# Last batch of an attention kernel: TensorE sums the last pieces of two halves, GpSimd and ScalarE put out two halves, the turned sums get buffers of their own, the last scores come in another order

## The chip, the cores and the metric

One core of one Trainium2 chip. The metric is the device time of one execution in microseconds (us); the time before is the median of three runs. TensorE is PE (its weight loads PEld), VectorE is DVE, ScalarE is ACT, GpSimd is POOL, and SyncE, which here only issues DMAs, is SP.

## The reference

For each of 32 images of 256 channels by 32x32 positions: a group normalisation (32 groups), projections to queries, keys and values of 8 heads with 32 channels each, attention in which a position sees only earlier positions, and the input added to the result. All in float32.

```python
q = einsum('oc,bcs->bos', q_w, gn(x)) + q_b;  kv likewise; k, v = split(kv)
scores = einsum('bhqd,bhkd->bhqk', q, k) / sqrt(32)          # S = 1024 positions
attn = softmax(where(mask == 0, -1e4, scores)); attn = where(mask == 0, 0, attn)
out = x + einsum('bhqk,bhkd->bhqd', attn, v)
```

## The kernel before

An image is a batch of the kernel. Its 8 heads are two groups g of four heads (128 channels), and its 1024 query positions are two halves hf of 512. So there are four halves per batch, n = 2g + hf = 0 to 3. Scores stand with the keys on the partitions: for a block of 128 keys, a head's scores are a 128x512 product. The exponentials (`e`, or `eh` where only 256 queries are concerned) are multiplied with the values into the numerator `acc`, and their sums over all keys are the denominators.

The program is a list of visits, 12 to a batch. Visit v of the last batch is program visit 372 + v, here written v0 to v12, v12 being the one after its last. The engines' order is written by hand (`manual_schedule`; SP's queue is not in it): each visit issues, in this order,

- its scores and exponentials and masks (`scores`: PE L269, ACT L324 twice and L322, POOL L283),
- the work listed in `at` for that visit (projections of the next image, L156, and so on),
- the products with the values of the visit before (`values`: PE L347), and on DVE the additions of those exponentials into one running sum per half (L353),
- the work listed in `after` for that visit.

Each engine works strictly in that order, so an instruction that waits holds everything behind it on its engine.

For all batches but the last, the running sum of a half is folded over the partitions by POOL's and SP's DMAs (`fold`, `stack`), turned and reduced on DVE (`sum_folded`, L382 and L383, two calls of two heads), inverted (`invert`), sent to memory and back as a broadcast tile `rb` (L425, L430), and used in `finish` (DVE L464, L465, for hf 0 also L467, then a DMA out from SP). For the batch before the last, `sum_folded` falls to v6 and v7, `invert` to v8, `finish` of its halves 0 and 1 to v10 and v11, and `finish_aside` of its halves 2 and 3 (POOL L475 and L476, ACT L477, for hf 0 L479, DMA) to v12.

The last batch has no time for that path. `sums` lets PE sum the running sum over the keys into `pd` (L390) and ACT copies it to `den` (L409); `invert_here` turns it on DVE (L450 into `turned`), checks its range (L413, L414 into `in_range`), inverts (L454) and spreads it (L455); `finish` follows. Halves 0, 1, 2 have `sums` at v3, v7, v9 and `invert_here` at v4, v8, v11; halves 0 and 1 have `finish` at v4 and v8. For half 3, `sums` comes at v11, the pieces of the last visit are summed by PE directly (`sum_piece` at v12), and `end_last` inverts it in two parts and puts out halves 3 and 2. At the end a minimum over `in_range` (L489) is summed by PE (L491) and decides whether a slower path has to run.

`den` and `turned` share one tag of the pool `small` with two buffers, in this order of use on their engines:

```python
turned = small.tile([P, HALF], F32, tag="den", ...)          # sum_folded, invert_here
live["den", n] = small.tile([P, HALF], F32, tag="den", ...)  # sums
```

PSUM has three 2-bank tiles for scores, one bank `acc`, and one bank `misc`, which `pd` shares with projections (`spare`). The tile of inverses of the last batch's half 0 has tag `rb` (4 buffers, shared with the batch before); those of halves 1 to 3 lie in `rb_last`.

In the last visit's scores, products of heads 2 and 3 for the short piece (`first`) come after the first block of the long piece, whose second block has only 128 queries.

Of the kernel before, what the change touches and what calls it, by code (L numbers as in the profile page):

```python
# [9 lines left out]
F32 = mybir.dt.float32  # L10
# [7 lines left out]
P = 128  # L18
HD = 32
# [12 lines left out]
def tile_norm_attention_residual(  # L32
# [54 lines left out]
    avg = avg.rearrange("p a b -> p (a b)")  # L87
    in_range = const.tile([P, ROW], F32, name="in_range")
    nc.gpsimd.memset(in_range, 1.0)
    eps = const.tile([P, 1], F32, name="eps")  # L90
    nc.gpsimd.memset(eps, 1e-5)

# [4 lines left out]
    def unshifted():  # L97
# [192 lines left out]
        def scores(b, full, half):  # L290


            tag = "e0" if full[2] == 0 else "e"
            name = f"{b}_{full[0]}_{full[1]}_{full[2]}"
            e = epool.tile([P, 4, HALF], F32, tag=tag, bufs=4 if tag == "e0" else 3, name=f"{tag}_{name}")
            eh = epool.tile([P, 4, HALFBANK], F32, tag="eh", bufs=4, name=f"eh_{name}")
            pairs = [ps_s.tile([P, 2, HALF], F32, tag="sT", name=f"sT_{name}_{a}") for a in range(3)]
            short = pairs[2].rearrange("p bank (n q) -> p bank n q", n=2)
            last = b == B - 1 and full[:2] == (NG - 1, NH - 1) and half[2] == NB - 2

            first = [] if last else [scores_of((b, half), short[:, j % 2, 1, :], j) for j in (2, 3)]


            for n in range(len(full[4])):
                for j in range(4):
                    scores_of((b, full), pairs[j // 2][:, j % 2, :], j, n)
                first = first or [scores_of((b, half), short[:, j % 2, 1, :], j) for j in (2, 3)]

            for ins in first:
                ins.then_inc(bank_free, 1)  # L310
                tc.no_tile_sem_insts.add(ins.ins.name)
            live["free"] = live.get("free", 0) + len(first)
            wait = nc.tensor.wait_ge(bank_free, live["free"])
            for ins in first:
                tc.declare_no_dep(wait.ins, ins.ins, reason="the semaphore orders them")
            for j in range(2):
                lo = scores_of((b, half), short[:, j, 0, :], j)
                for ins in first:
                    tc.declare_no_dep(lo.ins, ins.ins, reason="the semaphore orders them")
            for a in range(3):  # L320
                if a == 2:
                    exp = nc.scalar.activation(eh.rearrange("p (n bank) q -> p bank n q", n=2), short, AF.Exp)  # L322
                else:
                    nc.scalar.activation(e[:, 2 * a : 2 * a + 2, :], pairs[a], AF.Exp)  # L324

            for ins in first:
                tc.add_to_no_dep_group(f"first_{name}", ins.ins)
                tc.add_to_no_dep_group("first", ins.ins)
            tc.declare_no_dep(exp.ins, group=f"first_{name}", reason="through the last two products")
            tc.declare_fence(exp.ins, group=f"first_{name}")  # L330
            for heads in (range(2), range(2, 4)) if last else (range(4),):
                mask(full, e, slice(heads.start, heads.stop))
            mask(half, eh)
            live["e", b, full], live["e", b, half] = e, eh

        def values(b, pc, summed=True):
            g, hf, k, part, blocks = pc
            first, last = k == 0, k == hf * BPH + (1 if hf == 0 else 2)
            e = live.pop(("e", b, pc))
            if first:  # L340
                live["acc"] = ps_o.tile([P, HALF], F32, tag="acc", name=f"acc_{b}_{g}_{hf}")
                live["sum", b, g, hf] = e
            acc = live["acc"]
            for kb, cols, of in blocks:
                for j in range(4):
                    h = 4 * g + j
                    nc.tensor.matmul(  # L347
                        acc[HD * j : HD * (j + 1), of], lhsT=live["v", b][:, kb, h * HD : (h + 1) * HD],
                        rhs=e[:, j, cols], start=first, stop=last, skip_group_check=True,
                    )  # L350
                if not first and summed:
                    total = live["sum", b, g, hf]
                    nc.vector.tensor_add(total[:, :, of], total[:, :, of], e[:, :, cols])  # L353
            if last and (b, g, hf) == (B - 1, NG - 1, NH - 1):
# [22 lines left out]
        def sum_folded(b, heads):  # L377
            if heads.start == 0:
                live["rows", b] = small.tile([P, ROW], F32, tag="rows", name=f"rows_{b}")
            for j in heads:  # L380
                turned = small.tile([P, HALF], F32, tag="den", name=f"turned_{b}_{j}")
                nc.vector.transpose(turned, live["folded", b][:, j, :])  # L382
                nc.vector.tensor_reduce(  # L383
                    live["rows", b][:, j * HALF // HD : (j + 1) * HALF // HD],
                    turned.rearrange("p (k r) -> p k r", r=HD), AX.X, ALU.add,
                )
# [5 lines left out]
                    start=start, stop=stop, skip_group_check=True,  # L392
                )

        def sum_piece(b, pc, stop=False):

            e = live["e", b, pc]
            for kb, cols, of in pc[4]:
                sum_keys(live["den", 3], e, cols, of, False, stop)

        def sums(b, n):

            pd = misc(f"pd_{b}_{n}")
            sum_keys(pd, live.pop(("sum", b, *divmod(n, NH))), slice(0, HALF), slice(0, HALF), True, n < 3)
            if n == 3:
                live["den", n] = pd
            else:
                live["den", n] = small.tile([P, HALF], F32, tag="den", name=f"den_{b}_{n}")
                nc.scalar.copy(live["den", n], pd)  # L409

        def check_sums(rows):
            ok = in_range[:, : rows.shape[1]]
            nc.vector.scalar_tensor_tensor(ok, rows, SUM_MIN, ok, ALU.is_ge, ALU.mult)  # L413
            nc.vector.scalar_tensor_tensor(ok, rows, SUM_MAX, ok, ALU.is_le, ALU.mult)  # L414

        def invert(b):
            rows = live["rows", b]
            check_sums(rows)
            inv = small.tile([P, ROW], F32, tag="inv", name=f"inv_{b}")
            nc.vector.reciprocal(inv, rows)  # L420
            turned = small.tile([P, ROW], F32, tag="inv_turned", name=f"inv_turned_{b}")
# [21 lines left out]
        def invert_here(b, n, within=slice(0, HALF)):  # L443
# [2 lines left out]
            if within.start == 0:  # L446
                inverses(b, n)
            k = (within.stop - within.start) // HD
            turned = small.tile([P, HALF], F32, tag="den", name=f"turned_{b}_{n}_{within.start}")[:, : k * HD]
            nc.vector.transpose(turned, live["den", n][:, within])  # L450
            rows = turned.rearrange("p (k r) -> p k r", r=HD)[:, :, 0]
            check_sums(rows)
            inv = small.tile([P, ROW], F32, tag="inv", name=f"inv_{b}_{n}_{within.start}")[:, :k]
            nc.vector.reciprocal(inv, rows)  # L454
            nc.vector.transpose(  # L455
                live["rb", b, n][:, within].rearrange("p (k r) -> p k r", r=HD),
                inv.unsqueeze(2).broadcast_to([P, k, HD]),
# [9 lines left out]
                nc.vector.tensor_copy(rb[:, 0:1], xt[:, g, 0:1])  # L467
            nc.sync.dma_start(out=x_out[b, :, g, cols], in_=rb)

        def finish_aside(b, n):  # L470

            g, hf = divmod(n, NH)
            cols = slice(hf * HALF, (hf + 1) * HALF)
            rb, xt = live["rb", b, n], live["x", b]
            nc.gpsimd.tensor_tensor(rb, live["num", b, n], rb, ALU.mult)  # L475
            nc.gpsimd.tensor_tensor(rb, rb, xt[:, g, cols], ALU.add)  # L476
            nc.scalar.activation(rb, rb, AF.Identity, bias=v_bias_col[:, g : g + 1])  # L477
            if cols.start == 0:
                nc.scalar.copy(rb[:, 0:1], xt[:, g, 0:1])  # L479
            nc.sync.dma_start(out=x_out[b, :, g, cols], in_=rb)  # L480

        def end_last(b):

            both = [slice(c * HALFBANK, (c + 1) * HALFBANK) for c in range(2)]
            for part in both:
                invert_here(b, 3, part)

            worst = const.tile([P, 1], F32, name="worst")
            nc.vector.tensor_reduce(worst, in_range, AX.X, ALU.min)  # L489
# [47 lines left out]
        with tc.manual_schedule(engines={ENG.PE, ENG.Activation, ENG.DVE, ENG.Pool}):  # L537
# [31 lines left out]
            for b in range(B):  # L569
# [19 lines left out]
                elif not last:  # L589

                    for n in every[:2]:
                        when(first + N + 10 + n, lambda b=b, n=n: finish(b, n), after)
                    for n in every[2:]:
                        when(first + 2 * N, lambda b=b, n=n: finish_aside(b, n), after)
                else:
                    for n in every[:3]:
                        v = first + SUMS[n]
                        when(v, lambda b=b, n=n: sums(b, n), after)
                        v += 1 + n // 2
                        when(v, lambda b=b, n=n: invert_here(b, n), after)  # L600
                        if n < 2:
                            when(v, lambda b=b, n=n: finish(b, n), after)
            for i in range(B * N + 1):
                if i < B * N:
                    scores(i // N, *visits[i % N])
# [3 lines left out]
                if i == B * N:  # L609

                    for n, pc in enumerate(pcs):
                        sum_piece(B - 1, pc, stop=n == 1)
                for pc in pcs:
                    values((i - 1) // N, pc, i < B * N)
                if i == B * N - 1:
                    sums(B - 1, 3)
                for f in after.pop(i, ()):
                    f()
            assert not at and not after
# [158 lines left out]
```

## Time and profile before

| what | us |
|---|---|
| median of three runs | 1839.12 (1838.89 to 1840.98) |
| the profiled execution's own time | 1839.79 |
| its span | 1838.1 |
| PE busy / DVE busy / ACT busy / POOL busy | 1814.4 / 1663.4 / 1480.1 / 802.9 |
| mean granted TensorE clock | 0.993 |

The span runs from the first to the last instruction of one profiled execution; 1.69 us of the execution lie outside it, and the execution was 0.67 us over the median. The last batch's v0 starts at about 1756 us, v4 at 1775.8 and its last work on DVE ends at 1833.04; all the change is in that stretch. Busy shares over the whole span say little about it.

### The profile page before, as it was taken

The page shows a single profiled execution, that of the slowest core. Times are in us where ns is not written, and L with a number is a line of the kernel's source. Part 1 is how long each engine was busy: PE and PEld are TensorE (multiplying, and loading weights), DVE is VectorE, ACT ScalarE, POOL GpSimd, SP SyncE. Part 2 cuts the span into 40 slices and gives each one's busy share as a digit, 9 for nine tenths or more (in the row PEclk, how much of TensorE's full clock was granted, in tenths as well). Part 3 has the DMA queues.
Part 4 walks back from the last instruction along what each step waited for, and adds up shares of the span by engine and source line. Part 5 has one row for each costly group of instructions (what it writes and reads, how often), then busy time and mean ns, then how long its engine had stood idle before and what let it go on. Part 6 is the DMA issues. An engine that isn't in the chain of part 4 may idle for free.

```text
span 1838.1 us, 53791 instructions
## 1 busy us (share of the span) xinstructions
PE 1814.4 (99%) x23144; PEld 926.9 (50%) x23144; DVE 1663.4 (90%) x1774; ACT 1480.1 (81%) x1862; POOL 802.9 (44%) x779
## 2 busy tenths in 40 slices
PE   9999999999999999999999999999999999999995
PEld 5455555555555555554555555555545555555542
DVE  4799999999999999999999999999999999999988
ACT  5888878888878888888888788887888887888873
POOL 1453443534434434434445344354344454453432
PEclk9999999999999999999999999999999999999997
DMA  3457666676676666766676766667666767667651
GB/s 121 70 90 138 137 147 120 122 141 135 139 145 118 129 134 139 145 124 121 136 138 135 156 112 127 135 139 145 131 119 132 142 134 150 115 124 139 115 108 66
DMA packets 77781, 235.00 MB, mean 128 GB/s; under 512 B 20320, under 2 KB 21344, under 8 KB 61664
## 3 DMA queue, kind: packets, MB, share of 16 engines
q0 software_dynamic: 15872, 97.53, 38.7%
q1 hardware_dynamic: 61664, 133.96, 24.5%
q8 instruction: 183, 3.00, 0.7%
q14 instruction: 62, 0.51, 0.1%
HBM read 66.85 MB, written 34.57 MB: 55 GB/s over the span
## 4 chain that ended last, share of the span: by engine, by line
PE 97%; DVE 2%; issue 0%; DMA 0%; ACT 0%; DVEq 0%; ACTq 0%
PE sT L269 31%; PE acc L347 26%; PE pp L156 26%; PE ppv L156 13%; DVE e L353 1%; DVE rb L465 0%; DMA x<-in_x_dram 0%; PE pv L156 0%; PE pd L390 0%; DVE rb L464 0%; DVE st L166 0%; PE wt L135 0%; PE busy L142 0%; DVE turned L450 0%; PE pm L156 0%
## 5 line engine op out<-in xcount | busy, mean ns | idle before, releaser
L324 ACT ACTIVATE e<-sT 128x1024 f32<-128x1024 f32 x768 | 744.8, 1022 | 271.4 <-PE sT L269 213.2
L353 DVE TENSOR_TENSOR e<-e,e 128x1536 f32<-128x1536 f32 x382 | 642.3, 1681 | 17.9
L353 DVE TENSOR_TENSOR e<-e,eh 128x1024 f32<-128x1024 f32 x383 | 528.1, 1393 | 125.8 <-PE acc L347 105.3
L283 POOL TENSOR_SCALAR_AFFINE_SELECT e<-e 128x512 f32<-128x512 f32 (+1 forms) x257 | 378.5, 1473 | 575.9 <-ACT e L324 572.7
L269 PE MATMUL sT<-q,k 32*128 32x256 f32 (+3 forms) x7168 | 608.2, 459 | 0.0
L269 PEld LDWEIGHTS sT<-q,k 32*128 32x128 f32 x7168 | 445.3, 184 | 155.4 <-ACT eh L322 65.0
L156 PE MATMUL pp<-xn,wT 128*32 128x512 f32 x4096 | 494.0, 600 | 1.0 <-ACT den L409 1.0
L347 PE MATMUL acc<-e,v 128*32 128x512 f32 (+2 forms) x4096 | 401.2, 486 | 0.0
L322 ACT ACTIVATE eh<-sT 128x1024 f32<-128x1024 f32 x384 | 396.6, 1033 | 0.0
L369 POOL DMA_DIRECT2D e<-e x248 | 203.1, 823 | 388.9 <-DMA e<-e 306.5
L156 PE MATMUL ppv<-wT,xn 128*32 128x256 f32 x4096 | 247.5, 382 | 0.0
L347 PEld LDWEIGHTS acc<-e,v 128*32 128x32 f32 x4096 | 133.0, 110 | 224.6 <-issue 193.3
L347 PE MATMUL acc<-eh,v 128*32 128x256 f32 x3072 | 224.4, 379 | 0.0
L156 PEld LDWEIGHTS pp<-xn,wT 128*32 128x32 f32 x4096 | 107.2, 109 | 221.8 <-issue 206.5
L347 PEld LDWEIGHTS acc<-eh,v 128*32 128x32 f32 x3072 | 98.5, 110 | 164.2 <-issue 152.6
L156 PEld LDWEIGHTS ppv<-wT,xn 128*32 128x32 f32 x4096 | 120.1, 109 | 102.9 <-issue 30.8
L283 POOL TENSOR_SCALAR_AFFINE_SELECT eh<-eh 128x512 f32<-128x512 f32 x128 | 168.1, 1313 | 0.2
L209 ACT ACTIVATE xn<-x,shift,rstd 128x512 f32<-128x512 f32 x124 | 103.1, 831 | 0.0
L465 DVE SCALAR_TENSOR_TENSOR rb<-rb,v_bias_col,x 128x512 f32<-128x512 f32 x123 | 94.1, 765 | 4.4
L223 ACT ACTIVATE k<-pp,qk_bias 128x512 f32<-128x512 f32 x128 | 89.5, 700 | 3.2 <-PE pp L156 2.0
L223 ACT ACTIVATE q<-pp,qk_bias 128x512 f32<-128x512 f32 x128 | 89.8, 702 | 2.6 <-PE pp L156 2.6
L383 DVE TENSOR_REDUCE rows<-turned 128x16 f32<-128x512 f32 x124 | 85.0, 686 | 4.3
(70 smaller groups left out, 669.7 us busy)
## 6 DMA issues: line engine op xcount, KB each, us to landing
e<-e POOLq DMA_DIRECT2D x124, 512.0 KB, 6.2
x<-in_x_dram SPq DMA_DIRECT2D x64, 512.0 KB
out_dram<-rb SPq DMA_DIRECT2D x125, 256.0 KB
e<-e POOLq DMA_DIRECT2D x124, 256.0 KB, 4.8
folded<-e SPq DMA_DIRECT2D x124, 256.0 KB
rb<-inverses SPq DMA_DIRECT2D x124, 256.0 KB
inverses<-inv_turned SPq DMA_DIRECT2D x124, 8.0 KB
wn<-in_L_conv_kv_w_dram SPq DMA_DIRECT2D x2, 256.0 KB
```

Of the source, the lines that this page charges most:

```text
L156: nc.tensor.matmul(out[part], lhsT=lhsT[:, part], rhs=rhs, start=start, stop=stop, skip_group_check=True)
L209: nc.scalar.activation(xn, xt, AF.Identity, bias=live["shift", b][:, g : g + 1], scale=rstd)
L223: nc.scalar.activation(live[key][:, cols], pp, AF.Identity, bias=qk_bias[:, n, g : g + 1], scale=(SCALE, 1.0)[n],)
L269: return nc.tensor.matmul(pair[:, cols], lhsT=live["k", b, g][rows, kb * P : (kb + 1) * P], rhs=live["q", b, g][rows, hf * HALF + of.start ...
L283: nc.gpsimd.affine_select(out=diagonal, in_=diagonal, pattern=[[0, heads.stop - heads.start], [0, n], [1, P]], compare_op=ALU.is_gt, fill= ...
L322: exp = nc.scalar.activation(eh.rearrange("p (n bank) q -> p bank n q", n=2), short, AF.Exp)
L324: nc.scalar.activation(e[:, 2 * a : 2 * a + 2, :], pairs[a], AF.Exp)
L347: nc.tensor.matmul(acc[HD * j : HD * (j + 1), of], lhsT=live["v", b][:, kb, h * HD : (h + 1) * HD], rhs=e[:, j, cols], start=first, stop=l ...
L353: nc.vector.tensor_add(total[:, :, of], total[:, :, of], e[:, :, cols])
L369: nc.gpsimd.dma_start(out=total[:rows], in_=total[rows : 2 * rows], accum_op=ALU.add)
L383: nc.vector.tensor_reduce(live["rows", b][:, j * HALF // HD : (j + 1) * HALF // HD], turned.rearrange("p (k r) -> p k r", r=HD), AX.X, ALU ...
L465: nc.vector.scalar_tensor_tensor(rb, rb, v_bias_col[:, g : g + 1], xt[:, g, cols], ALU.add, ALU.add)
```

## The change

In the last batch:

- `values` no longer adds on DVE at v6 (the last pieces of half 1), v11 and v12 (the last of half 3; v12 was without already). `sums(1, products[5])` at v7 and `sums(3, pcs)` at v11 let PE sum those pieces from their exponentials, beside the running sum.
- `invert_here` of half 0 moves from v4 to v6 (ahead of the products), of half 2 from v11 to v10; half 1's stays at v8.
- Halves 0 and 1 are put out by `quotient_aside` (POOL, at v7 and v8) and `out_aside` (ACT and DMA, at v8 and v10) in place of `finish` on DVE.
- `turned` has a tag with two buffers of its own, `den` has one.
- The range check of the four halves becomes one over their inverses, 128x64, in `end_last`.
- `finish` of halves 0 and 1 of the batch before moves from v10 and v11 to v11, both.
- In the last visit the two short products come after half of the long piece's second block.

```diff
+    inv_last = const.tile([P, 4, HALF // HD], F32, name="inv_last")
@@ scores
+                long_of(range(4), 0)
+                long_of((0, 1), 1)
+                first = short_of((2, 3), 1)
+                long_of((2, 3), 1)
@@ values
-                if not first and summed:
+                if not summed:
+                    continue
+                if not first:
                     total = live["sum", b, g, hf]
                     nc.vector.tensor_add(total[:, :, of], total[:, :, of], e[:, :, cols])
@@ sum_folded, invert_here
-                turned = small.tile([P, HALF], F32, tag="den", ...)
+                turned = small.tile([P, HALF], F32, tag="turned", ...)
@@ sums
+        def sums(n, pcs=()):
+            live["pd"] = misc(f"pd_{n}")
+            sum_keys(live["pd"], live.pop(("sum", B - 1, *divmod(n, NH))), ..., n < 3 and not pcs)
+            for k, pc in enumerate(pcs):
+                sum_piece(pc, n < 3 and k == len(pcs) - 1)
...
+                live["den", n] = small.tile([P, HALF], F32, tag="den", bufs=1, name=f"den_{n}")
@@ invert_here
-            check_sums(rows)
-            nc.vector.reciprocal(inv, rows)
+            inv = inv_last[:, n, within.start // HD : within.stop // HD]
+            nc.vector.reciprocal(inv, turned.rearrange("p (k r) -> p k r", r=HD)[:, :, 0])
@@ quotient_aside, out_aside (finish_aside in two)
+            nc.gpsimd.tensor_tensor(rb, live["num", b, n], rb, ALU.mult)
+            nc.gpsimd.tensor_tensor(rb, rb, live["x", b][:, g, hf * HALF : (hf + 1) * HALF], ALU.add)
...
             nc.scalar.activation(rb, rb, AF.Identity, bias=v_bias_col[:, g : g + 1])
@@ end_last
+            check(inv_last.rearrange("p n k -> p (n k)"), 1.0 / SUM_MAX, 1.0 / SUM_MIN)
@@ the program
-                        when(first + N + 10 + n, lambda b=b, n=n: finish(b, n), after)
+                        when(first + N + 11, lambda b=b, n=n: finish(b, n), after)
...
-                    for n in every[:3]:
-                        v = first + SUMS[n]
-                        when(v, lambda b=b, n=n: sums(b, n), after)
-                        v += 1 + n // 2
-                        when(v, lambda b=b, n=n: invert_here(b, n), after)
-                        if n < 2:
-                            when(v, lambda b=b, n=n: finish(b, n), after)
+                    when(first + 3, lambda: sums(0), after)
+                    when(first + 7, lambda: sums(1, products[5]), after)
+                    when(first + 9, lambda: sums(2), after)
+                    for n, v in enumerate((6, 8, 10)):
+                        when(first + v, lambda b=b, n=n: invert_here(b, n), (at, after)[n > 0])
+                    for n in every[:2]:
+                        when(first + 7 + n, lambda b=b, n=n: quotient_aside(b, n), after)
+                        when(first + 8 + 2 * n, lambda b=b, n=n: out_aside(b, n), after)
@@
-                    values((i - 1) // N, pc, i < B * N)
+                    values((i - 1) // N, pc, i - (B - 1) * N not in (6, 11, 12))
                 if i == B * N - 1:
-                    sums(B - 1, 3)
+                    sums(3, pcs)
```

## The prediction

> **What bounds the kernel now.** First the page: PE is busy 99% of the span, so only what stops PE, or what lies behind PE's last work, can be worth anything. The chain of waits is PE until v4 of the last batch and then leaves it. These are its pieces (start, length, what):
>
> ```profile
> 1779.20 1.09 PE acc L347 x13
> 1780.30 1.51 DVE e L353
> ...
> 1794.06 1.24 DVE e L353
> 1795.30 0.04 issue
> 1795.34 1.98 PE pd L390 x8
> ...
> 1799.75 0.70 DVE rows L383
> ...
> 1800.55 0.59 ACT den L409
> 1801.15 0.04 issue
> 1801.19 3.64 PE pp L156 x16
> ```
>
> From 1780.30 to 1833.04, DVE's end, the chain is mostly DVE. PE's `pd` at v7 waits for DVE's last addition of v6; then ACT's copy of `pd` waits for a reduction (L383) that has nothing to do with its data. The answer on the tile `turned` names that wait, 7.5 us, once: the copy's buffer is one of the two that `turned` uses too. Behind it on ACT stand v8's exponentials, and behind the bank `misc` PE's projection.
>
> The stretches of time (PE, PEld, DVE, ACT, POOL busy with counts, granted clock, DMA share, GB/s) show the price:
>
> ```profile
> 1788.00:1791.70 3.70, 3.70 (x44) 1.77 (x40) 3.49 (x3) 3.13 (x5) 2.50 (x3) 1.00 0.01 2
> 1791.70:1795.30 3.60, 0.04 (x4) 0.00 (x0) 3.46 (x4) 1.33 (x2) 1.23 (x1) 0.89 0.00 0
> 1795.30:1801.20 5.90, 4.82 (x26) 2.00 (x26) 5.76 (x9) 0.65 (x2) 0.00 (x0) 0.50 0.00 0
> 1801.20:1804.70 3.50, 3.50 (x20) 0.88 (x24) 3.38 (x6) 2.70 (x3) 0.00 (x0) 0.50 0.05 9
> 1804.70:1816.90 12.20, 12.17 (x140) 5.79 (x132) 11.73 (x16) 9.63 (x12) 2.00 (x2) 1.00 0.28 104
> 1816.90:1820.80 3.90, 0.00 (x0) 0.00 (x0) 3.80 (x3) 0.80 (x1) 3.90 (x3) 1.00 0.23 87
> 1820.80:1833.10 12.30, 5.53 (x58) 2.39 (x58) 11.74 (x26) 1.64 (x3) 6.30 (x5) 0.68 0.21 78
> ```
>
> PE stands still for 3.60 us, then runs at half clock until 1804.7 (16 projections take 3.64 us, 1.86 elsewhere), and stands still again for 3.9 us at v11. DVE has almost no idle time in any row.
>
> **What the skill says.** The Trainium skill, "TensorE: Matmul & The Clock Gate", What's actually happening: after an idle window of about 3.4 us PE runs at half clock until it has been busy for as long. The trace agrees: clock 0.50 behind the wait of 3.60 us; gaps under 1.1 us in the chain don't do it. "SBUF — State Buffer", SBUF: two separate sides: a GpSimd operation and a DVE operation with two SBUF inputs exclude each other for a whole instruction. The trace shows interference, not that it is total: beside POOL's L475 and L476 two DVE checks of 128x16 took 0.51 and 1.21 us, 0.18 elsewhere. "GPSIMD Engine Reference", Engine selection: two-input elementwise work is about twice as slow there; here 1.49 us (mean of L475) against DVE's 0.69 (L464).
>
> **DVE's part.** From the timeline of DVE, starts to next start:
> - v6's additions go: 1790.41 to 1795.30, 4.9 us. v11's go: 1816.74 to 1820.78, 4.0.
> - output of half 0 goes (L464, L465, L467): 1783.80 to 1786.19, 2.4; of half 1: 1807.40 to 1808.80, 1.4.
> - range checks go: 0.32, 0.32, 1.75 (the one slowed by POOL), 0.36, 0.37, together 3.1; one check of 128x64 comes, as at 1801.81: 0.4.
>
> Sum 15.4 us less on DVE. Were DVE never to wait and never slowed, it would end at 1833.04 - 15.4 = 1817.6. That is the floor.
>
> **PE's and ACT's part.** Until v7's products end (1791.7) PE doesn't wait for DVE and nothing changes. `sums(1)` now needs the running sum only through v5. DVE is through with that at 1781.8 + 3.8 = 1785.6, because half 0's inversion and output no longer stand ahead of it (1781.73 to 1786.19). So `pd` starts at 1791.7: 0.86 us for the running sum (the chain's pd x8 of 512 columns at full clock) and 1.29 for 768 columns of pieces, to 1793.9. ACT ended v7's exponentials at 1793.0; with its own buffer the copy runs at once, to 1794.5. **Both waits go, and with them the reason for the half clock.** Next, with durations of full-clock rows:
> - v8: scores 1.5, projection 1.86, products 0.87: PE at 1798.1. ACT: exponentials 1795.05 (1.2 behind the scores, as at v4 and v6) to 1797.9, `k` and `num` to 1799.05, then the new L477 and L479 (0.72 + 0.19) to 1800.0. Their wait is for POOL's half 0, which starts behind v7's mask (1793.4) and takes 1.49 + 1.43, up to 3.3: 1796.7 at the latest, so no wait.
> - v9: exponentials 1800.0 to 1802.8, 0.7 later than without the new pair, and v10's short scores wait for that bank: PE loses 0.7. Products 1.72, `pd` 0.86, copy to 1803.4.
> - v10: scores to 1804.35, exponentials to 1806.9, products to 1805.6; then L477 of half 1 to 1807.6. POOL has half 1 ready at 1800.5 + 3.3 = 1803.8.
> - v11: scores (bank free at 1806.9) to 1807.9; exponentials 1807.6 to 1810.45; products to 1809.2; `sums(3)` with 768 columns of pieces (2.15) to 1811.35. The new order of scores lets pair 0 go some 0.3 us earlier, which ACT's L477 hides: I cost it at nothing, and if that cover were gone it would gain up to 0.3.
> - v12: three masks on POOL. Alone 0.94 each and 1.1, contended 1.88, 1.88 and 1.65 as at 1815.93: they end between 1811.6 and 1814.0. The pieces' sums behind them: `pd` is complete at about 1813.7.
>
> DVE beside it, from 1785.6: inversion 0 1.75, first fold turn 2.75, v7's addition (waits for `acc` to 1791.1) 1.2, second turn 2.75, `invert` 1.15, v8's additions 2.45, inversion 1 1.75, v9's 2.4, v10's 3.8, inversion 2 1.75, `finish` of two halves 3.0: 1811.4. Two things slow it. POOL's four new operations last 5.8 us; in v12 of before, POOL's four (1821.3 to 1827.25) cost DVE 2.7 (inversion 2 took 3.4 instead of 2.05, a `finish` 2.8 instead of 1.45), so 2.7; masks some 0.5. DVE is then free at 1814.6, 0.9 later than `pd`. The sum for half 3 isn't delayed: v10's additions end at 1809.4 at worst against 1809.2.
>
> **The end.** `end_last` took 1826.85 to 1833.04, 6.2; minus 0.73 of checks plus 0.4 is 5.9. It now lies wholly beside POOL's last four operations, where only 0.4 of it did: plus 2.7. DVE ends at 1814.6 + 8.6 = 1823.2. POOL's last output (1814.0 + 6.0, ACT 0.7) is at 1820.7, earlier. Behind DVE's end come 5.06 us to the span's end as before: 1828.3. With 1.69 outside, 1830.0 against this execution's 1839.79: 9.8 less; on the median, 1829.3. Rounding toward the floor's side, since a part of the POOL slowdown was counted at its worst: **1829.0 us**, a likeliest range of 1824 to 1833. Without any contention `pd` would be complete at 1812.2 and DVE end 5.9 later, 1818.1: 1824.2 on the median.
>
> **What costs nothing, and its cover.** `rb` has four buffers, and half 0's stays in use until v8's DMA out, while the batch before asks for four at v8: one of its four broadcasts (L430) must wait for that DMA. It lands by 1800.5 + 5 (5.06 is the bound that the end of the span gives), the broadcast takes at most the 10.2 us from 1804.90 to its use at 1815.09: 1815.7. If it is half 3's, POOL wants it at about 1817 and nothing waits; if half 0's, `finish` at v11 waits up to 5 us. SP's order is not written by hand, so I keep that in the range. Holding `e` of v5 until v7 costs nothing: its buffer comes round at v10.
>
> **Rivals.** (a) GpSimd's lock is total for its new work. Then the eight POOL operations cost DVE their whole 11.7 us instead of 5.4: 1829.0 + 6.3 = 1835.3; half of it, or a late broadcast, gives 1832 to 1834. For it: the 1.21 us check. Against: two DVE transposes beside them (L450, L455) kept their 0.70. (b) **Slower**: ACT's L477 of half 1 stands ahead of v11's exponentials and waits for POOL. Every us that POOL ends half 1 after 1806.9 is added to exponentials, masks, sums and end. From 1817 on the gain is used up; with POOL starved to 1820, 1842. Against: POOL's operations took at most 1.69 with DVE busy throughout, and would need five times that. (c) The waits go, but DVE stays behind PE at `sums(2)` and `sums(3)`, PE idles over 3.4 us there and falls to half clock again: about 6 us back and the `pd` of v12 twice as long, 1837, which a measurement cannot tell from no change (0.2%, 3.7 us, is about its limit).
>
> **Numbers.** Likeliest case 0.77, (a) 0.13, (c) 0.04, (b) 0.06. Faster by over 0.2%: 0.90; within: 0.04; slower: 0.06. The range reaches from the uncontended 1824 to most of (a): 1824.0 to 1834.5.
>
> **What would show it.** Right: no PE wait for L353 at v7 and none of ACT for L383; clock near 1.0 until v12; `pd` at v7 with 32 products; v8's projection at 1.9 us; DVE's additions 5 fewer; DVE idle for less than 2 us ahead of half 3's inversion; span near 1827. Wrong: DVE idle for long at v8 to v11 (ACT or POOL is the bound), an idle PE of over 3 us anywhere before v12, an L430 issued long after the other three, or DVE operations doubled beside L475.

## The result, and the profile after

| | before | changed | ratio (95% interval) |
|---|---|---|---|
| median of six runs each, us | 1839.63 (1838.79 to 1840.98) | 1828.07 (1827.45 to 1829.07) | 0.9938 (0.9925 to 0.9950) |
| profiled execution: time, span, us | 1839.79, 1838.1 | 1827.53, 1825.8 | |
| from v4's first scores product to the end of the span, us | 62.33 | 51.52 | |

The forecast was 1829.0, within 1824.0 to 1834.5. The last row is the one to compare kernels by. Of the 12.3 us between the two spans, 1.49 lie before v4 (scores at 1775.77 and 1774.28), where the change has no work. They are not the change's: three variants of the changed kernel that are profiled below (with the old order of scores, without POOL's work of v12, and with v10's pieces on PE and another buffer) began v4 at 1775.75 to 1776.06, as the kernel before did. PE's clock between 9 and 12 us of the span was 0.55 in one of the two profiles and 1.00 in the other; in the fourteen profiles of this case it was 0.51 to 0.60 in seven, with v4 at 1775.7 to 1776.1, and 1.00 in seven, with v4 at 1774.2 to 1774.6 in all but one. So the change is worth 10.81 us in the profiles. The stretch from v4's first scores product to the end of the span is called the tail below.

The changed kernel has other line numbers for the same work: L356 stands for L347 of before (products with the values), L364 for L353 (additions), L393 and L394 for L382 and L383, L401 for L390 (`pd`), L425 for L409 (copy to `den`), L445 for L430 (broadcasts), L465, L467 and L468 for L450, L454 and L455 (inversion), L477, L478 and L480 for L464, L465 and L467 (`finish`), L487 and L488 for L475 and L476 (POOL), L494 for L477 (ACT), L428 and L429 for the checks L413 and L414.

The stretches of the changed kernel (PE, PEld, DVE, ACT, POOL busy with counts, clock, DMA share, GB/s). All times in it are 1.49 us earlier than in the kernel before for the same work:

```profile
1788.00:1791.70 3.70, 3.70 (x55) 1.70 (x52) 2.79 (x4) 2.97 (x4) 1.39 (x2) 1.00 0.02 7
1791.70:1795.30 3.60, 3.60 (x52) 1.84 (x45) 3.46 (x7) 2.36 (x3) 2.94 (x3) 1.00 0.00 0
1795.30:1801.20 5.90, 5.90 (x78) 2.81 (x70) 5.76 (x9) 5.87 (x10) 1.29 (x1) 1.00 0.19 62
1801.20:1804.70 3.50, 3.50 (x44) 1.89 (x36) 3.40 (x2) 3.04 (x5) 3.42 (x3) 1.00 0.33 124
1804.70:1809.40 4.70, 4.04 (x46) 1.92 (x44) 4.53 (x5) 3.47 (x5) 4.70 (x4) 1.00 0.18 63
1809.40:1813.00 3.60, 3.60 (x64) 1.74 (x56) 3.53 (x5) 0.00 (x0) 3.52 (x3) 1.00 0.38 126
1813.00:1820.80 7.80, 0.45 (x10) 0.12 (x2) 7.42 (x19) 1.64 (x3) 3.10 (x3) 0.80 0.44 160
```

PE is busy without a break until 1804.7 and idle for 0.66 us after that, the clock is 1.00 to 1813.0, PE's last products but a few, and ACT, which did 0.65 us in 5.9 before, now does 5.87. The chain of waits of the changed kernel (start, length, what) shows where it leaves PE now:

```profile
1790.25 2.15 PE pd L401 x32
1792.41 1.50 PE sT L270 x12
1793.91 1.85 PE pp L157 x16
...
1799.75 3.40 DVE e L364 x2
...
1803.25 3.19 DVE e L364
...
1810.36 1.66 DVE rb L478
...
1812.20 1.51 DVE rb L477
...
1814.49 0.37 DVE turned L465
```

`pd` of v7 follows PE's products at once, with 32 products in 2.15 us, and v8's projection takes 1.85 (3.64 before). From 1799.75, the additions at v9, the chain is DVE to DVE's end, 21.1 us of it. Its length is not its work: two additions of 128x1024 that took 2.35 us in the kernel before, with POOL idle, took 3.40. The timelines of before (two lines) and of the changed kernel (four) show these additions and those that follow, with POOL's work on half 1 beside them:

```profile
1808.80 2.35 DVE L353 TENSOR_TENSOR e<-e,eh 128x1024 f32<-128x1024 f32 x2
1811.26 2.29 DVE L353 TENSOR_TENSOR e<-e,e 128x2048 f32<-128x2048 f32 x1
...
1799.75 3.40 DVE L364 TENSOR_TENSOR e<-e,eh 128x1024 f32<-128x1024 f32 x2
1799.91 2.15 POOL L487 TENSOR_TENSOR rb_last<-num,rb_last 128x512 f32<-128x512 f32 x1 [5.19 <-DVE rb_last L468]
1802.14 2.14 POOL L488 TENSOR_TENSOR rb_last<-rb_last,x 128x512 f32<-128x512 f32 x1
1803.25 3.18 DVE L364 TENSOR_TENSOR e<-e,e 128x2048 f32<-128x2048 f32 x1
```

### The profile page after: what moved, and what is told of

Its sections match the earlier page's. It is cut to its first block, busy times and chain, and to the rows that moved or that the text cites. A ratio compares the mean times of both kernels' runs of the same rounds, so it can differ in the third digit from the quotient of the medians.

```text
span 1825.8 us, 53853 instructions
## 1 busy us (share of the span) xinstructions
PE 1809.1 (99%) x23184; PEld 925.3 (51%) x23184; DVE 1652.5 (91%) x1756; ACT 1481.7 (81%) x1865; POOL 808.8 (44%) x783
## 3 DMA queue, kind: packets, MB, share of 16 engines
q0 software_dynamic: 15872, 97.53, 38.8%
## 4 chain that ended last, share of the span: by engine, by line
PE 98%; DVE 1%; DMA 0%; ACT 0%; issue 0%; DVEq 0%
PE sT L270 31%; PE acc L356 27%; PE pp L157 26%; PE ppv L157 13%; DVE e L364 0%; DMA x<-in_x_dram 0%; PE pv L157 0%; PE pd L401 0%; DVE st L167 0%; DVE rb L478 0%; DVE rb L477 0%; PE pm L157 0%; DVE rb_last L478 0%; DVE rb_last L468 0%; PE busy L143 0%
## 5 line engine op out<-in xcount | busy, mean ns | idle before, releaser
L364 DVE TENSOR_TENSOR e<-e,e 128x1536 f32<-128x1536 f32 (+1 forms) x379 | 636.9, 1680 | 17.8
L364 DVE TENSOR_TENSOR e<-e,eh 128x1024 f32<-128x1024 f32 x381 | 526.9, 1397 | 124.9 <-PE acc L356 104.1
L356 PE MATMUL acc<-e,v 128*32 128x512 f32 (+2 forms) x4096 | 400.7, 486 | 0.7 <-POOL e L284 0.7
L356 PEld LDWEIGHTS acc<-e,v 128*32 128x32 f32 x4096 | 132.6, 110 | 224.0 <-issue 191.4
L356 PE MATMUL acc<-eh,v 128*32 128x256 f32 x3072 | 224.4, 379 | 0.0
L356 PEld LDWEIGHTS acc<-eh,v 128*32 128x32 f32 x3072 | 98.5, 110 | 164.2 <-issue 153.2
L478 DVE SCALAR_TENSOR_TENSOR rb<-rb,v_bias_col,x 128x512 f32<-128x512 f32 x122 | 92.7, 760 | 4.4
L394 DVE TENSOR_REDUCE rows<-turned 128x16 f32<-128x512 f32 x124 | 85.1, 686 | 4.3
```

The source lines that it names most:

```text
L356: nc.tensor.matmul(acc[HD * j : HD * (j + 1), of], lhsT=live["v", b][:, kb, h * HD : (h + 1) * HD], rhs=e[:, j, cols], start=first, stop=l ...
L394: nc.vector.tensor_reduce(live["rows", b][:, j * HALF // HD : (j + 1) * HALF // HD], turned.rearrange("p (k r) -> p k r", r=HD), AX.X, ALU ...
L478: nc.vector.scalar_tensor_tensor(rb, rb, v_bias_col[:, g : g + 1], xt[:, g, cols], ALU.add, ALU.add)
```

## The experiments

All tails are from v4's first scores product, as PE's timeline has it, to the end of the span, in one profile each. The stretch behind DVE's last instruction alone took 4.72 to 5.28 us in them, so a difference of a few tenths of a us says nothing by itself; the table at the end of this section gives DVE's end too. The expectations of the first four that were run (buffers, sums, both, outputs on DVE) name 62.26 and 51.45, counted from the same point in the chain of waits, 0.07 us later. The medians of the timed runs stand in the same table.

**Buffers alone**

```diff
-turned = small.tile([P, HALF], F32, tag="den", ...)      # in sum_folded and invert_here
+turned = small.tile([P, HALF], F32, tag="turned", ...)
-live["den", n] = small.tile([P, HALF], F32, tag="den", ...)
+live["den", n] = small.tile([P, HALF], F32, tag="den", bufs=1, ...)
```

> The kernel before, with nothing changed but that turned has two buffers of its own and den has one. Measured from v4's first scores product to the end of the span: 62.26 us before, 51.45 in the changed kernel. Theory (DVE's total work from v4 on sets the end; the copy's wait for L383 is one of two waits in the same DVE-bound stretch): the wait of ACT for L383 goes (7.5 us to none) and PE's projection of v8 starts about 1 us earlier, but PE still waits 3.6 us for L353 at v7 and DVE has as much work as before: 61.5 to 62.3, gain under 0.8. Rival (the two waits and the half clock are themselves the cost): gain of 3 us or more, under 59.3.

Tail 63.86, 1.53 longer than before, neither the theory's number nor the rival's. ACT's wait for L383 went, PE came to v11's end some 3.4 us earlier, and then stood there. Behind the same wait of 3.60 us at v7 the clock did not fall this time: it was 1.00 from there to the end of v11's products. Behind the wait at v11 it did fall, and the `pd` of v11 took 4.5 us; DVE, busy until then, did not wait for it. The timeline of that kernel, first PE's sums of v7 and v11 (start, length, what, and in brackets the idle time before and what ended it), then DVE and POOL in v11 and v12:

```profile
1795.31 1.06 PE L390 MATMUL pd<-e,pick 128*32 128x512 f32 x8 [3.60 <-DVE e L353]
1823.21 3.64 PE L390 MATMUL pd<-e,pick 128*32 128x512 f32 x24 [9.77 <-DVE e L353]
```

```profile
1817.80 3.16 DVE L353 TENSOR_TENSOR e<-e,e 128x2048 f32<-128x2048 f32 x1
1818.89 3.19 POOL L476 TENSOR_TENSOR rb<-rb,x 128x512 f32<-128x512 f32 x1
1821.06 2.10 DVE L353 TENSOR_TENSOR e<-e,eh 128x1024 f32<-128x1024 f32 x1
1822.04 2.25 POOL L475 TENSOR_TENSOR rb<-num,rb 128x512 f32<-128x512 f32 x1
```

With DVE as late as ever, PE only waited longer (9.77 us), and POOL's work of v12, which follows PE and ACT, came early enough to run beside DVE's additions of v11: 3.16 and 2.10 us instead of 2.54 and 1.47. A stall taken away in front of a busy engine moved POOL's work onto it. The medians of the timed runs can't tell this kernel from the one before.

**PE's sums alone**

```diff
-values((i - 1) // N, pc, i < B * N)
+values((i - 1) // N, pc, i - (B - 1) * N not in (6, 11, 12))
-sums(b, n)                # v7
+sums(b, n, products[5])
-sums(B - 1, 3)            # v11
+sums(B - 1, 3, pcs)
# left out here: the lines that keep these exponentials and hand them to sum_piece
```

> The kernel before, with nothing changed but that PE sums the pieces of v6 (half 1) and v11 (half 3), which DVE no longer adds. Theory (DVE's total sets the end): DVE loses 8.9 us of additions, so v4 to the end takes about 62.26 - 8.9 = 53.4 (52.5 to 54.5), and the shared buffer costs next to nothing, since L383 comes 4.9 us earlier too: ACT's wait for L383 shrinks from 7.5 us to 2 to 3. Rival (the shared buffer is the stall that counts): ACT's copy still waits long, PE falls to half clock, and v4 to the end stays over 56.

Tail 53.69: 8.64 shorter, against 8.9 us of additions taken from DVE. ACT's copy waited for the buffer as expected, 2.78 us, and PE 1.05 us for the copy, with no fall of the clock before the end of PE's work:

```profile
1796.05 0.59 ACT L414 COPY den<-pd 128x512 f32<-128x512 f32 x1 [2.78 <-DVE rows L385]
```

**Both** (the two edits above together)

> The kernel before with both: buffers of turned's own, and PE's sums of the pieces of v6 and v11; outputs, range checks, times of the inversions and order of the scores as before. Theory: within 0.8 us of the kernel with PE's sums alone, 52.5 to 54 from v4 to the end, so that outputs on POOL and ACT, the single check and the moved inversions are together worth 1 to 2.5 of the 10.8. Rival: as in the run with PE's sums alone, the buffers are worth over 2 once PE's wait is gone.

Tail 53.91. The buffers are worth nothing beside PE's sums either: the tail is 0.22 us longer, DVE's end 0.11 earlier.

**Outputs alone, in the kernel before**

```diff
-if n < 2:
-    when(v, lambda b=b, n=n: finish(b, n), after)
+when(first + 7 + n, lambda b=b, n=n: quotient_aside(b, n), after)   # n = 0, 1
+when(first + 8 + 2 * n, lambda b=b, n=n: out_aside(b, n), after)
# left out here: finish_aside in two, as in the change
```

> The kernel before, with nothing changed but that halves 0 and 1 of the last batch are put out by POOL and ACT, at the places that the change gives them. Theory (DVE's total less what POOL's two-input operations take from it): DVE loses 3.8 us and gets 1.5 to 2.7 back as slower instructions; v4 to the end 62.33 - 1.1 to - 2.3: 60.0 to 61.3; PE still waits at v7 and v11, ACT for L383. Rival (the outputs were not on the path while PE and ACT waited): 62.0 to 62.6.

Tail 62.50, the rival's number: nothing gained. The theory's price was too low. DVE lost 3.8 us of `finish` and got it back: v9's additions took 3.83 us (2.35 before) beside POOL's half 1, v11's second 2.10 (1.47), `finish` of the batch before 2.13 and 3.40 (1.43 and 2.81), and DVE waited 0.82 us for `acc`, which PE had late: ACT's copy waited 5.55 us for L383 and PE's projection 4.09 us for the copy. The rival's reason, that the outputs were not on the path, is at most that last part of what the trace shows. It also shows that the shared buffer can cost something once DVE has less to do.

**The changed kernel with the outputs on DVE**

```diff
-when(first + 7 + n, lambda b=b, n=n: quotient_aside(b, n), after)
-when(first + 8 + 2 * n, lambda b=b, n=n: out_aside(b, n), after)
+when(first + 6 + 2 * n, lambda b=b, n=n: finish(b, n), (at, after)[n > 0])
```

> The changed kernel, with halves 0 and 1 put out by finish on DVE (at v6 and v8, behind their inversions) in place of POOL and ACT. Theory: DVE gets 3.8 us back, but loses what POOL's half 1 costs it (additions of v9 and v10: 3.40 and 3.18 us instead of 2.35 and 2.28) and PE's wait of 0.65 us for a mask held up behind POOL's half 1; v4 to the end 51.45 + 0.3 to + 2, that is 51.8 to 53.5. Rival (POOL's help is free): + 3.8, 55.2. Second rival (POOL's help costs more than it gives): under 51.2.

Tail 53.67, 2.15 longer, just above the theory's range. So in the changed kernel POOL's and ACT's help gives 2.15 of the 3.8 us it takes from DVE. This kernel differs from the one with both parts only in the single range check, the places of inversions and `finish`, and the order of the scores: together 0.24.

**The old order of the last scores**

```diff
 long_of(range(4), 0)
-long_of((0, 1), 1)
 first = short_of((2, 3), 1)
-long_of((2, 3), 1)
+long_of(range(4), 1)
```

> The changed kernel with the last visit's scores in the order of before (the short pair behind the first block of the long piece). Times from v4's first scores product, as the timeline of PE has it, to the end of the span: 62.33 us before, 51.52 in the changed kernel. Theory (DVE sets the end from v9 on, and v11's exponentials wait for ACT's L494 of half 1 rather than for the scores): 51.3 to 51.8, no difference. Rival (the masks behind the exponentials still count): + 0.3 or more.

Tail 51.65, 0.13 longer: no difference that one profile can tell.

**Without POOL's work of v12**

```diff
-when(first + 2 * N, lambda b=b, n=n: quotient_aside(b, n), after)
-when(first + 2 * N, lambda b=b, n=n: out_aside(b, n), after)
+when(first + 2 * N, lambda b=b, n=n: live.pop(("rb", b, n)), after)
```

> The changed kernel without the output of halves 2 and 3 of the batch before the last: POOL's four operations of v12, ACT's three and two DMAs out are left out, so these parts of the output are not written. DVE's own instructions are all there. Theory (POOL's two-input operations hold up DVE's, which set the end): DVE's finish of two halves at v11 shrinks from 4.8 us towards 3.0 and the rest of the end by some 0.3, so v4 to the end takes 49.3 to 50.2 instead of 51.52. Rival (DVE's slow instructions there have another cause, or the end is set by the DMAs out): 51.2 to 51.8 or, if the DMAs out count, a shorter stretch between DVE's last instruction and the end, 4.97 us in the changed kernel.

Tail 49.57, 1.95 shorter, and DVE's last instruction is followed by 5.08 us, so the DMAs out were not it. Two halves of the batch before are not written by this kernel. Here are DVE's two `finish` in the timeline of the changed kernel and then of this one:

```profile
1809.63 0.70 DVE L477 TENSOR_TENSOR rb<-num,rb 128x512 f32<-128x512 f32 x1
1810.36 1.65 DVE L478 SCALAR_TENSOR_TENSOR rb<-rb,v_bias_col,x 128x512 f32<-128x512 f32 x1
...
1812.12 1.58 DVE L477 TENSOR_TENSOR rb<-num,rb 128x512 f32<-128x512 f32 x1
1813.74 0.75 DVE L478 SCALAR_TENSOR_TENSOR rb<-rb,v_bias_col,x 128x512 f32<-128x512 f32 x1
```

```profile
1811.28 0.70 DVE L477 TENSOR_TENSOR rb<-num,rb 128x512 f32<-128x512 f32 x1
1812.02 0.75 DVE L478 SCALAR_TENSOR_TENSOR rb<-rb,v_bias_col,x 128x512 f32<-128x512 f32 x1
...
1812.87 0.68 DVE L477 TENSOR_TENSOR rb<-num,rb 128x512 f32<-128x512 f32 x1
1813.59 0.75 DVE L478 SCALAR_TENSOR_TENSOR rb<-rb,v_bias_col,x 128x512 f32<-128x512 f32 x1
```

The same instructions, 4.7 us against 2.9. Nothing but POOL's (and behind it ACT's and the DMAs') work was taken away. This run doesn't part the three; the times speak for POOL: each of the slow instructions lies beside an operation of POOL's, and ACT's first output of v12 began only at 1813.19 in the changed kernel. The timed runs (median 1827.88) show much less of the gain than the profile.

**One more visit's pieces on PE**

```diff
-values((i - 1) // N, pc, i - (B - 1) * N not in (6, 11, 12))
+values((i - 1) // N, pc, i - (B - 1) * N not in (6, 10, 11, 12))
-sums(3, pcs)
+sums(3, products[9] + pcs)
```

> The changed kernel with one more visit's additions taken from DVE: the pieces of v10 (half 3, 768 columns) are summed by PE in v11's pd too, 1.3 us more on PE, 4.8 us of additions less on DVE. Theory (DVE is the bound by about 2.5 us, then PE's pd): DVE is free at about 1809.7 on the changed kernel's clock, pd is complete at about 1813.2 instead of 1811.95, so half 3's inversion starts some 1.2 us earlier than 1814.41: 50.0 to 50.9 from v4 to the end. Rival (DVE is the bound by more than its work shows): gain of 3 or more, under 48.5. Second rival (PE or ACT is already the bound): 51.5 or more.

Tail 51.18, only 0.34 shorter, which the theory (50.0 to 50.9) missed. The inversion of half 3 did start earlier, 38.31 us behind v4 instead of 40.13, with DVE idle for 4.50 us ahead of it and waiting for `pd`. But from there to DVE's end it took 7.59 us instead of 6.47, and behind DVE's end 5.28 us followed instead of 4.92. POOL's last pair had to wait 2.96 us for the late fourth broadcast (L445 here, from SP) and so ran beside DVE's end, as the timeline shows:

```profile
1808.74 0.51 SPq L445 DMA_DIRECT2D rb<-inverses  x1
...
1814.76 1.26 POOL L487 TENSOR_TENSOR rb<-num,rb 128x512 f32<-128x512 f32 x1 [2.96 <-DMA rb<-inverses]
1814.89 1.21 DVE L429 SCALAR_TENSOR_TENSOR in_range<-inv_last,in_range 128x64 f32<-128x64 f32 x1
```

**Half 1 alone on DVE**

```diff
+if n:
+    when(first + 8, lambda b=b, n=n: finish(b, n), after)
+    continue
 when(first + 7 + n, lambda b=b, n=n: quotient_aside(b, n), after)
```

> The changed kernel with half 1 alone put out by finish on DVE at v8, half 0 still by POOL and ACT. With both halves on DVE v4 to the end took 53.67 against 51.52. Theory: half 1 costs DVE 1.4 and spares it what POOL's half 1 cost the additions of v9 and v10 (3.40 and 3.18 us instead of 2.35 and 2.3) and PE 0.65 of a mask: 51.5 to 52.9. Rival (POOL's half 1 takes more from DVE than it gives): under 51.2.

Tail 52.14, 0.62 longer. The additions of v9 and v10 were back at 2.35 and 2.29 us, and the inversion started 0.42 earlier, but POOL's last pair again waited for the broadcast, 2.44 us, and one check took 1.31: the end took 7.47 us.

**A buffer that the fourth broadcast needn't wait for**

```diff
-tag="rb", bufs=4
+tag="rb" if b < B - 1 else "num", bufs=4 if b < B - 1 else 8    # half 0's inverses
```

> The changed kernel with a buffer for half 0's inverses that no broadcast of the batch before has to wait for (one of the eight of num). In the changed kernel the fourth broadcast (L430) was issued at 1808.47, 8.9 us behind the third's end, and POOL's last pair waited 0.77 us for it. Theory (that broadcast's cover held but for the 0.77 us of POOL, which is not what ends last): fourth broadcast issued with the others, POOL's wait gone, v4 to the end 51.52 to within 0.5: 50.9 to 51.8. Rival (the late broadcast costs the end): under 50.8.

Tail 52.43, 0.91 longer: neither theory's number. The four broadcasts were issued together and POOL's wait of 0.77 us was gone, so its last pair started at 1813.02 and met DVE's second `finish`, whose L478 took 1.64 us instead of 0.75. That wait had kept POOL out of DVE's way.

**That buffer, and v10's pieces on PE**

> The changed kernel with the pieces of v10 summed by PE too and with that buffer. With the pieces alone half 3's inversion started 1.8 us earlier, but the end behind it took 7.59 us instead of 6.47: POOL's last pair waited 2.96 us for the late broadcast and then ran beside it (a check took 1.21). Theory: with the broadcast early POOL is through before; the inversion starts at 38.3 behind v4 as in that run, the end takes 6.0 to 6.4, 5.0 follow: 49.3 to 49.9. Rival (the end's slowness has another cause, or the DMAs out end last): 50.8 or more.

Tail 49.44, as expected, 2.08 shorter than the changed kernel. In the timeline DVE now waits for `pd`, and POOL's last operation is beside the transposes and over before the first check:

```profile
1814.38 0.45 DVE L465 STREAM_TRANSPOSE turned<-pd 128x256 f32<-128x256 f32 x1 [4.50 <-PE pd L401]
...
1814.95 1.27 POOL L488 TENSOR_TENSOR rb<-rb,x 128x512 f32<-128x512 f32 x1
...
1816.52 0.18 DVE L428 SCALAR_TENSOR_TENSOR in_range<-inv_last,in_range 128x64 f32<-128x64 f32 x1
1816.74 0.22 DVE L429 SCALAR_TENSOR_TENSOR in_range<-inv_last,in_range 128x64 f32<-128x64 f32 x1
```

**And half 1 on DVE besides**

> As the run before it, and half 1 put out by DVE. DVE sat idle for 4.5 us ahead of half 3's inversion once the pieces of v10 were PE's, so 1.44 us more of work is hidden, POOL's masks come sooner, and pd is complete 0.4 us earlier as it was with half 1 on DVE in the changed kernel (37.27 against 37.68 behind v4). Theory: 48.8 to 49.6. Rival (DVE is then the bound again): 50 or more.

Tail 49.64, not under the theory's 49.6. DVE has the room (it still waits 3.87 us for `pd`), but `pd` was no earlier: 38.24 us behind v4 in both. The 0.4 us counted on didn't come.

| kernel | median, us | ratio to before (95%) | tail, us | DVE's end behind v4, us |
|---|---|---|---|---|
| before | 1839.63 | | 62.33 | 57.27 |
| changed | 1828.07 | 0.9938 (0.9925 to 0.9950) | 51.52 | 46.60 |
| buffers alone | 1841.00 | 1.0004 (0.9995 to 1.0013) | 63.86 | 58.91 |
| PE's sums alone | 1831.43 | 0.9953 (0.9936 to 0.9970) | 53.69 | 48.97 |
| both | 1830.68 | 0.9951 (0.9934 to 0.9968) | 53.91 | 48.86 |
| outputs alone | 1838.95 | 0.9997 (0.9988 to 1.0006) | 62.50 | 57.49 |
| changed, outputs on DVE | 1831.38 | 0.9953 (0.9937 to 0.9970) | 53.67 | 48.63 |
| changed, old order | 1829.02 | 0.9940 (0.9923 to 0.9956) | 51.65 | 46.79 |
| changed, no POOL work of v12 | 1827.88 | 0.9934 (0.9917 to 0.9950) | 49.57 | 44.49 |
| changed, v10 on PE | 1827.39 | 0.9936 (0.9919 to 0.9952) | 51.18 | 45.90 |
| changed, half 1 on DVE | 1829.61 | 0.9945 (0.9928 to 0.9962) | 52.14 | 47.18 |
| changed, other buffer | 1828.20 | 0.9937 (0.9920 to 0.9953) | 52.43 | 47.19 |
| changed, v10 on PE, other buffer | 1826.24 | 0.9925 (0.9908 to 0.9941) | 49.44 | 44.49 |
| changed, both of these, half 1 on DVE | 1827.32 | 0.9932 (0.9915 to 0.9948) | 49.64 | 44.48 |

Each ratio is to runs of the kernel before that were made together with it. The intervals of the kernels near the changed one overlap; between them the tails and the durations in them tell more than the medians.

## Why the prediction was right, point by point

**PE at v7** was right: `pd` follows the products at once (15.79 us behind v4, predicted 15.93), the copy runs at once, the clock stays at 1.00 (but see the last section on the 3.4 us that the prediction has for the clock).

**PE and ACT to v12** were right in sum: `pd` complete 37.68 us behind v4, predicted 37.9. ACT's two outputs caused no wait of ACT for POOL. One wait wasn't seen: the mask of v10 stood behind POOL's half 1, and PE's products of v11 waited 0.65 us for it. The 0.7 us that PE was to lose at v10's scores did not come, so the sum is right in part by luck.

**The 15.4 us less on DVE** was the right term to look at, and the experiments say so: of the parts, PE's sums alone bring 8.64 of the 10.81, what they take from DVE. But the prediction told the gain twice, as two stalls with a half clock and as DVE's work, and left open which one pays. The runs settle most of it: without ACT's wait for L383, and without the half clock behind v7, nothing was gained (63.86); beside PE's sums the buffers gained nothing either (53.91 against 53.69); and PE's sums, which end the wait of 3.60 us and the half clock, brought no more than the work they take from DVE. No run ends PE's wait at v7 and leaves DVE its work, so that one wait is not tried by itself. The bold sentence that both waits go was true, but it is not where the time came from.

**What POOL takes from DVE** was mis-sized in both places, with opposite signs. Up to half 3's inversion 2.7 us and 0.5 for masks were counted, and 4.4 came: v9's additions 1.05, v10's 0.9, two `finish` 1.8, a check of the batch before 0.7. Operations doubled beside POOL's, a sign of being wrong by the prediction's own list, were among them (L478 1.65 us instead of 0.75). DVE was free 40.13 us behind v4, predicted 38.8. In the end 2.7 us more were counted, on 5.9, and `end_last` took 6.47 instead of 8.6; it takes 6.16 with POOL idle, in the run without its work of v12, so 0.3 came. The first pair of POOL's last four operations fell on the `finish` instead, and the last pair mostly on transposes and reciprocals, which kept their times (0.45 and 0.20 us at most beside it, 0.45 and 0.20 with POOL idle). DVE ended 46.60 us behind v4, predicted 47.4. The sum was good to 0.8 us because two errors of 1.3 and 2.1 cancel, which is luck.

**The broadcast** (L430) was listed as a sign of being wrong, and it came: the fourth was issued 8.9 us behind the third. Its cover held all the same, as POOL waited 0.77 us for it, off the path; and with its own buffer the tail was longer. The sign was a bad one: it told of a wait, not of what waits behind it.

**The range check.** Of its 3.1 us, 1.75 were one check slowed by POOL. Taking the slowed instruction away left the slowing to others (in the changed kernel with the outputs on DVE the two `finish` took 6.2 us, in the kernel with both parts 5.4); check, places and order together brought 0.24.

**The order of the scores** at nothing: 0.13.

Rival (b), slower through ACT's wait for POOL, had nothing to it: POOL's half 1 was ready at 1804.28, ACT came to it at 1804.69, 0.4 us later. That was nearer than predicted (3 us): POOL took 4.4 us, not 3.3, and began 0.9 later, and ACT came 0.7 earlier. Rival (a) has the lock right and its price wrong. The times at v9 and v10 fit a total lock (last section), yet the new work and v12's cost DVE about 4.7 us, not 11.7, and less than the 5.9 that the likeliest case counted with its masks.

## What to carry to other kernels

Where one engine is busy without a break to the end, price an edit by what it takes from that engine: here the end of a visible stall of 7.5 us and of 9.4 us of half clock was worth nothing, and 8.9 us of additions moved to an engine with room were worth 8.6. Work given to GpSimd comes back in part as slower two-input work on VectorE, so price it by what will stand beside it, and expect any edit that makes GpSimd earlier to change that. When two parts hinder each other, as the late broadcast and the earlier inversion here (tails 0.34 shorter and 0.91 longer alone, 2.08 shorter together), single trials mislead.

## What the runs showed of the hardware that was not expected

A GpSimd operation and a VectorE operation with two inputs in SBUF take turns by whole instructions. At v9 of the changed kernel the first of DVE's two additions had begun when POOL's product came, and kept its 1.2 us; POOL's product took 2.15 us instead of 1.27, DVE's second addition 2.29 instead of 1.2 (it began at 1800.86), POOL's next operation 2.14, and DVE's addition of 128x2048 3.18 instead of 2.29. Each grew by 0.87 to 1.07 us, and of the operation that it met 1.0 to 1.2 us were left. So both engines lose, each in turn. This is what the Trainium skill says in "SBUF — State Buffer", SBUF: two separate sides: of the two, the one that starts first has the shared ports for its whole instruction, and the other is blocked. The prediction found the lock not shown to be total by the kernel before; these times fit a total one. An operation of POOL's that met a long addition took 3.19 us with the buffers alone and 3.28 with the outputs alone. Transposes of 128x512 took at most 0.71 us in the last batch of all fourteen profiles, beside POOL or not.

TensorE's clock did not follow the 3.4 us that the prediction has for its fall and its return. In the kernel before, read in stretches of 0.6 us, it fell 2.8 us into the wait of 3.60 us at v7, and at v11 only 4.9 us after PE had stopped, when PE was at work again behind 3.96 us. With the buffers alone it stayed at full through the wait of 3.60 us and fell 4.0 us into that of 9.77; with the outputs alone it fell 3.9 and 4.8 us into waits of 4.09 and 6.33 us. It came back 3.2 to 5.3 us after PE's return in four of these five cases, and after 9.4 us in the one at v7, where PE worked for 4.8 us at half clock, stood for 1.04 and worked again. So a wait of this length can go either way, and one profile doesn't tell which way a kernel goes.

A DMA that waits for a buffer can wait long. The fourth broadcast was issued 8.9 us after the third; for 8.1 us of that SP waited for the output of 256 KB from the same buffer. The output was issued behind the three broadcasts, and from 1799 to 1808.5 the DMA engines, with a mean busy share of 0.30, moved 1.06 MB, about what the three broadcasts and the output, 256 KB each, have together. How long the output would take alone wasn't measured.
